# Five matmul rounds instead of six for a channel polynomial, and GpSimd products over two images at once, in a convolution and attention kernel

## The chip, the cores and the metric

The kernel runs on one core of a Trainium2 chip. The metric is the device time of one execution in microseconds. TensorE multiplies matrices into PSUM, VectorE and ScalarE read and write PSUM and SBUF, GpSimd works on SBUF alone, and SyncE (SP) issues DMAs. All data is float32.

## The reference

Two layers over 32 images of 64 channels and 56 x 56 pixels (3136 pixels, called N).

Layer 0 works in 8 groups of 8 channels. In each group, at each pixel, it forms all products of two channels (36) and of three (120), and mixes each set with a learned matrix:

```python
p2 = x[:, :, _I2] * x[:, :, _J2]
y2 = jnp.einsum('bgihw,goi->bgohw', p2, W2).reshape(B, Ch, H, Wd) + b2[None, :, None, None]
p3 = x[:, :, _I3] * x[:, :, _J3] * x[:, :, _K3]
y3 = jnp.einsum('bgihw,goi->bgohw', p3, W3).reshape(B, Ch, H, Wd) + b3[None, :, None, None]
return inp + y2 * beta2 + y3 * beta3 * CONV3_SCALE
```

Layer 1 is an attention over pixels, with a small convolution behind it:

```python
g = jnp.clip(_bn(conv1x1(l, w_inside), ...), 0.0, 6.0)
theta = l[:, :c_red]                            # 32 of the 64 channels
f = jnp.einsum('niab,nicd->nabcd', theta, theta)
f = softmax(f, over the first pixel index); f = softmax(f, over the second)
out = jnp.einsum('nabcd,nicd->niab', f, g) / h * w
out = _bn(depthwise_conv3x3(out, w_dw), ...)
return out + l
```

## The kernel before

**Pairs and tiles.** The images go two at a time, in 16 pairs (`NP`). The 64 channels of image 0 and of image 1 of a pair lie on the two halves of the 128 partitions of `y`, three of which are kept in turn (`ys`). The 3136 x 3136 attention matrix of an image is made in tiles of 128 rows (`QT`), 24 for each image and one for the two remainders: 49 tiles a pair (`IT`), 784 in all. The loop at the end of the kernel body runs over tiles `t`. A tile has two halves. `scores(t, half)` multiplies `theta` with itself into four PSUM banks (tile `ps`, a single buffer), and VectorE copies the half to `e` in SBUF, with a running minimum in `nm`. ScalarE then takes the exponential of the whole tile (`first_softmax`), and of that once more (`second_softmax`, one tile later). Three tiles later (`LAG`), `attend` multiplies the rows of `e` with `g` (tiles `gq`, `gx`) into the accumulators `av` and `ax`: 25 blocks of two matmuls, `split(t)` of them in the first half of a tile, the others in the second.

**The polynomial as matmuls.** The host stores each group's channels in rotated order and extends them (`EXT` rows), so that "channel i + d" of all channels is one load that starts d rows further on. A product of two channels, one d apart, needs two such loads and an elementwise multiply; all pairs with the same d (an orbit) are then a product of 32 partitions (8 channels of 4 groups, half an image). Four orbits stand above one another on 128 partitions (`NSLOT`), and one matmul contracts them all. `STEPS` lists, for each slot, the quadratic orbit a and the cubic ones that go with it. For a piece of half an image (index `k`, 0 to 3 for the four halves of a pair) round 0 contracts `q = x0 * xa` (the four quadratics), rounds 1 to 4 contract `q` times the loads "0", "2", "4" and "b" (the cubics). The last quadratic orbit, channels 4 apart, has no slot left: it is a sixth round of its own (`NRND` is 5, so `r == NRND`), from the loads `c`, multiplied by GpSimd over both images, 128 partitions, with the weights `w4`.

**Chunks.** The pixels of a pair go in 13 chunks of 242 (`PCS`, the last one of 232). In `products`, GpSimd multiplies, for each chunk and `k`, one product of 128 x 242 a round (20 in all), and one for `c`. The products land in rings (`ring_q`, `ring_pr`; `ROOM`), and the loads come from rings `x0`, `xs`, `xc` (`XB`), which SP fills in the order of `plan`, as far as slots are free (`held`) and as `PACE` allows. The first image (two halves) is made before the loop by VectorE, in seven chunks of 448 columns (`first_loads`, `first_products`, `first_poly`), and the second image of the first pair (`TWO`) in the loop, in chunks of 484 columns (`DCS`), one half image at a time.

**Units beside the attention.** While pair n is attended to, the polynomial of pair n + 1 is computed. `rounds` cuts the rounds of a chunk into units: two rounds a unit (`per`), three in the stretch of `TWO`. `poly` issues a unit's matmuls into a free part of the bank `ax`; behind the last unit `poly_out` adds bias and input on VectorE, to `y`. `g_unit` makes a part of `g` in the same place. Each unit has a half tile (`hs`), and a weight of 1 + 3.6 for each round; `split` gives the half with less of such work more attention blocks. The 3 x 3 convolution of pair n - 1 is done by VectorE at the same time: 45 steps (`conv_step`, `scalar_tensor_tensor` over `tt` and `y`) in half tiles in which no unit ends (`leaves`). GpSimd adds a bias ahead of each block of it (`conv_begin`).

**Order.** Each engine runs its instructions in the order of the program (`Pinned`). Waits between engines are put in from the tiles that are read and written. All matmuls, products and loads stand on one line of the profile, L110 (L111 in the kernel after).

Of the kernel before, what the change touches and what calls it, by code (L numbers as in the profile page):

```python
# [19 lines left out]
N = H * W  # L20
# [31 lines left out]
    (0, [0, 2, 4, 5]),  # L52
    (1, [0, 2, 4, 1]),
    (2, [0, 2, 4, 5]),
    (3, [0, 2, 4, 1]),
# [3 lines left out]
NRND = 5  # L59
NPROD = sum(1 + len(bs) for _, bs in STEPS)  # L60
# [11 lines left out]
def tile_poly_conv_attention(  # L72
# [60 lines left out]
    w4 = const.tile([128, 128], FP, name="w4")  # L133
    at = 0
    for s, (_, bs) in enumerate(STEPS):
        for h in range(2) if s < NSLOT else ():
            act.dma_start(
                out=wq[s::NSLOT, :, h, :],
                in_=wpoly[h * 32 : h * 32 + 32, at : at + NRND, h * 32 : h * 32 + 32],
            )  # L140
        if s == NSLOT:
            act.dma_start(out=w4, in_=wpoly[:, at, :])
        at += 1 + len(bs)
# [14 lines left out]
    for k in range(2):  # L158
        pe.matmul(
            out=ax[:, k * 256 : k * 256 + 256],  # L160
            lhsT=w4,
            rhs=wq.rearrange("p k h o -> p (k h o)")[:, :256],
            start=(k == 0),
            stop=True,
            skip_group_check=True,
        )
# [39 lines left out]
    def parts(tiles):  # L206
# [10 lines left out]
        "0": [(0, 1, 0, 0)],  # L217
        "a": [(0, 1, 0, 1)],
        "2": [(0, 1, 2, 0)],
        "4": [(0, 1, 4, 0)],  # L220
        "b": [(0, 2, 5, 0), (1, 2, 1, 0)],
    }

    def first_loads(c):
        p0, w = FCS[c]

        def load(dst, k, d, grow, steps):
            src = bass.AP(x.tensor, (k * EXT + d) * 4 * N + p0, [[N, 32], [grow * 4 * N, steps], [1, w]])
            if steps == 1:
                src = bass.AP(x.tensor, (k * EXT + d) * 4 * N + p0, [[N, 32], [1, w]])  # L230
            (act if fat["q"] % 2 else sync).dma_start(out=dst, in_=src)
            fat["q"] += 1

        fxs[c] = {}
        for name, k in [(a, k) for k in (0, 1) for a in "0a"] + [(a, k) for a in "24b" for k in (0, 1)]:
            t = fx[fat["x"] % len(fx)]
            fat["x"] += 1
            fxs[c][name, k] = t
            for s0, every, d, grow in LOADS[name]:
                load(t[s0::every, :] if every > 1 else t, k, d, grow, NSLOT // every)  # L240
        for d in (0, 1):
            t = fx[fat["x"] % len(fx)]
            fat["x"] += 1
            fxs[c]["c", d] = t[:C, :]
            for k in (0, 1):
                load(t[k * 32 : k * 32 + 32, :], k, 4 * d, 0, 1)

    def first_products(c):
        xs = fxs[c]

        def product(a, b):
            p = fp[fat["p"] % len(fp)]
            fat["p"] += 1
            dve.tensor_tensor(p, a, b, ALU.mult)
            return p

        q = {k: product(xs["0", k], xs["a", k]) for k in (0, 1)}
        frs[c] = [q] + [{k: product(q[k], xs[a, k]) for k in (0, 1)} for a in "024b"]
        dve.tensor_tensor(xs["c", 1], xs["c", 0], xs["c", 1], ALU.mult)
        frs[c].append(dict.fromkeys((0, 1), xs["c", 1]))  # L260
# [8 lines left out]
    for k in range(NRND):  # L269
        by = row("beta2_0") if k == 0 else b3row  # L270
        w = wq[:, k, :, :].rearrange("p h o -> p (h o)")
        dve.tensor_tensor(w, w, by, ALU.mult)
    for half in (0, C):
        w = w4[:, half : half + C]
        dve.tensor_tensor(w, w, row("beta2_0"), ALU.mult)
# [25 lines left out]
    XB = {"x0": 6, "xs": 14, "xc": 3}  # L301
# [12 lines left out]
    ringc = xp.tile([128, 2 * XB["xc"] * PCH], FP, name="ring_xc", tag="xc", bufs=1)  # L314
# [7 lines left out]
    def take_ring(tag, w):  # L322
        t, at = ring[tag]
        m, size = many(w), t.shape[1]
        if at % m or at + m > size:
            at = 0
        ring[tag][1] = (at + m) % size
        return t[:, at : at + m, :].rearrange("p m w -> p (m w)")[:, :w]

    def load_next():  # L330
        tag, key = plan.pop(0)
        n, c, ks, name, k = key
        p0, w = chunks(ks)[c]
        if name[0] == "c":
            held[tag] += 1
            sub = int(name[1:])
            p0, w = p0 + sub * PCH, min(PCH, w - sub * PCH)
            o = fat["c"] % XB["xc"] * 2 * PCH
            fat["c"] += 1
            t = ringc[:, o : o + 2 * PCH].rearrange("p (d w) -> p d w", d=2)  # L340
            at = slice(ks[0] * 32, ks[-1] * 32 + 32)
            for d in range(2):
                src = bass.AP(
                    x.tensor,
                    ((4 * n + ks[0]) * EXT + 4 * d) * 4 * N + p0,
                    [[EXT * 4 * N, len(ks)], [N, 32], [1, w]],
                )
                start(t[at, d, :w], src)
            loaded[key] = [t[at, d, :w] for d in range(2)]
            return  # L350
        held[tag] += many(w)
        t = take_ring(tag, w)
        for s0, every, d, grow in LOADS[name]:
            src = bass.AP(
                x.tensor,
                ((4 * n + k) * EXT + d) * 4 * N + p0,
                [[N, 32], [grow * 4 * N, NSLOT // every], [1, w]],
            )
            start(t[s0::every, :] if every > 1 else t, src)
        loaded[key] = t  # L360

    def prefetch():
        while plan and credit[0] >= 1:
            tag, (_, c, ks, _, _) = plan[0]
            m = 1 if tag == "xc" else many(chunks(ks)[c][1])
            if held[tag] + m > XB[tag]:
                return
            load_next()
# [6 lines left out]
    def products(n, c, ks):  # L375
# [5 lines left out]
        m = many(w)  # L381

        def use(name, k=None):
            key = n, c, ks, name, k
            return loaded.pop(key)

        x0 = {}
        rounds = [{}]
        both = []
        prods[n, c, ks] = rounds, both  # L390
        yield "q", m * len(ks)
        for k in ks:
            yield "load", (n, c, ks, "a", k)
            x0[k] = use("0", k)
            xa = use("a", k)
            q = take_ring("q", w)
            pool.tensor_tensor(q, x0[k], xa, ALU.mult)
            rounds[0][k] = q
            held["xs"] -= m
            prefetch()  # L400
        for r, of in enumerate(("0", "2", "4", "b")):
            rounds.append({})
            yield "pr", m * len(ks)
            for k in ks:
                if of != "0":
                    yield "load", (n, c, ks, of, k)
                xr = x0[k] if of == "0" else use(of, k)
                p = take_ring("pr", w)
                pool.tensor_tensor(p, rounds[0][k], xr, ALU.mult)
                rounds[-1][k] = p  # L410
                held["x0" if of == "0" else "xs"] -= m
                prefetch()
        at = slice(ks[0] * 32, ks[-1] * 32 + 32)
        yield "pr", m
        p4 = take_ring("pr", w)[at, :]
        for sub in range(m):
            yield "load", (n, c, ks, f"c{sub}", None)
            both.append(use(f"c{sub}"))
            pool.tensor_tensor(p4[:, sub * PCH : min((sub + 1) * PCH, w)], *both[sub], ALU.mult)
        rounds.append({k: p4 for k in ks})  # L420
# [26 lines left out]
    def feed(n, c, ks):  # L447
        todo = [("x0" if name == "0" else "xs", name, k) for k in ks for name in "0a"]
        for name in "24bc":
            if name == "c":  # L450
                todo += [("xc", f"c{sub}", None) for sub in range(many(chunks(ks)[c][1]))]
            else:
                todo += [("xs", name, k) for k in ks]
        for tag, name, k in todo:
            plan.append((tag, (n, c, ks, name, k)))
# [18 lines left out]
    def poly(n, c, ks, rs, sub):  # L474
# [4 lines left out]
        at = slice(ks[0] * 32, ks[-1] * 32 + 32)  # L479
        for r in rs:  # L480
            for k in ks:
                pe.matmul(
                    out=ax[k * 32 : k * 32 + 32, AUX : AUX + w],
                    lhsT=wq[:, r, k % 2, :] if r < NRND else w4[at, k * 32 : k * 32 + 32],
                    rhs=rounds[r][k][:, px],
                    start=False,
                    stop=(r == NRND),
                    skip_group_check=True,
                )
            if ends:  # L490
                taken["pr" if r else "q"] -= (sub + 1) * (1 if r == NRND else len(ks))

    def poly_out(n, c, ks, sub):
# [4 lines left out]
        xc = prods[n, c, ks][1][sub][0]  # L498
# [210 lines left out]
    def make_diags():  # L709

        eye = take_ring("xs", 128)
# [5 lines left out]
        for k in range(9):  # L717
            t = take_ring("xs", 128)
# [82 lines left out]
    def poly_unit(n, c, ks, rs, sub, hs):  # L801
        ends = rs[-1] == NRND
# [29 lines left out]
    def first_poly(c):  # L832
        p0, w = FCS[c]
        for r in range(NRND + 1):
            for k in (0, 1):
                pe.matmul(
                    out=banks[c][k * 32 : k * 32 + 32, :w],
                    lhsT=wq[:, r, k, :] if r < NRND else w4[:C, k * 32 : k * 32 + 32],
                    rhs=frs[c][r][k],
                    start=(r == 0),  # L840
                    stop=(r == NRND),
# [3 lines left out]
    def first_out(c):  # L845
        p0, w = FCS[c]
        dve.scalar_tensor_tensor(
            ys[0][:C, p0 : p0 + w], banks[c][:C, :w], bias0[:C], fxs[c]["c", 0], ALU.add, ALU.add
        )
# [68 lines left out]
    for n in range(NP):  # L918
# [4 lines left out]
        def rounds(m, c, ks, per):  # L923
            return [
                ("p", m, c, ks, list(range(r, r + per)), sub)
                for sub in range(many(chunks(ks)[c][1]))
                for r in range(0, NRND + 1, per)
# [202 lines left out]
```

## Time and profile before

| | us |
|---|---|
| device time, median of 3 runs | 4951.68 (4951.55 to 4952.49) |
| profiled execution, span | 4946.9 |
| TensorE busy | 4722.0 (95%) |
| ScalarE busy | 4553.9 (92%) |
| VectorE busy | 4120.5 (83%) |
| GpSimd busy | 3208.4 (65%) |
| loop, first pair (start of ScalarE's first tile to the second pair's) | 381.5 |
| loop, pairs 1 to 14, each | 293.3 to 294.0 |
| loop, last pair | 282.0 |

The profiled execution's own time is its span with what lies around it; the span is 4.8 us shorter than the median. A row of the profile names engine, operation, the tiles written and read (out<-in, without buffer numbers), partitions x elements, the number of instructions, their busy time (overlaps counted once) and the mean duration of one. A float32 matmul leaves two records. Matmuls on different columns of the array overlap, so the busy time of a group divided by its count is less than the duration of one.

### The profile page before, as it was taken

The page shows a single profiled execution, that of the slowest core. Times are in us where ns is not written, and L with a number is a line of the kernel's source. Part 1 is how long each engine was busy: PE and PEld are TensorE (multiplying, and loading weights), DVE is VectorE, ACT ScalarE, POOL GpSimd, SP SyncE. Part 2 cuts the span into 40 slices and gives each one's busy share as a digit, 9 for nine tenths or more (in the row PEclk, how much of TensorE's full clock was granted, in tenths as well). Part 3 has the DMA queues.
Part 4 walks back from the last instruction along what each step waited for, and adds up shares of the span by engine and source line. Part 5 has one row for each costly group of instructions (what it writes and reads, how often), then busy time and mean ns, then how long its engine had stood idle before and what let it go on. Part 6 is the DMA issues. An engine that isn't in the chain of part 4 may idle for free.

```text
span 4946.9 us, 263995 instructions
## 1 busy us (share of the span) xinstructions
PE 4722.0 (95%) x118122; PEld 3215.6 (65%) x118122; DVE 4120.5 (83%) x6100; ACT 4553.9 (92%) x2356; POOL 3208.4 (65%) x4275
## 2 busy tenths in 40 slices
PE   4998999999999999999999999999999999999887
PEld 1555666666666666666666666666666666666665
DVE  4655898888988898888889889888888889888887
ACT  0777899999999999999999999999999999999996
POOL 1777685858758586785858768585875858678000
PEclk8999999999999999999999999999999999999999
DMA  6555656565565655556565555656555565554201
GB/s 203 152 148 153 146 144 155 145 151 141 138 145 145 152 147 143 147 145 144 149 145 147 147 146 142 150 145 152 146 140 141 150 147 146 145 147 125 45 11 34
DMA packets 875486, 685.65 MB, mean 139 GB/s; under 512 B 289772, under 2 KB 860524, under 8 KB 870252
## 3 DMA queue, kind: packets, MB, share of 16 engines
q1 hardware_dynamic: 865964, 657.85, 52.0%
q8 instruction: 924, 15.14, 1.3%
q10 hardware_dynamic: 8384, 10.91, 0.7%
q14 instruction: 214, 1.75, 0.1%
HBM read 565.65 MB, written 25.69 MB: 120 GB/s over the span
## 4 chain that ended last, share of the span: by engine, by line
PE 78%; DVE 11%; issue 3%; DMA 3%; ACT 3%; POOL 1%; SPq 1%; ACTq 0%; DVEq 0%; POOLq 0%
PE av L110 33%; PE ps L110 26%; PE ax L110 19%; DVE e L110 9%; ACT e L110 3%; DMA ring_xs<-in_x_dram 2%; POOL ring_pr L110 1%; DVE y L110 1%; DVE num L110 1%; SPq L110 1%; DMA ring_xc<-in_x_dram 1%; DMA first<-in_x_dram 1%; PE first_s L110 0%; DMA th<-y 0%; POOL ring_q L110 0%
## 5 line engine op out<-in xcount | busy, mean ns | idle before, releaser
L110 PEld LDWEIGHTS av<-gq,e 128*64 128x64 f32 x64512 | 2011.4, 138 | 943.1 <-issue 936.1
L110 ACT ACTIVATE e<-e,nm 128x3136 f32<-128x3136 f32 x784 | 2282.9, 2912 | 235.2 <-DVE e L110 219.6
L110 ACT ACTIVATE e<-e,rz 128x3136 f32<-128x3136 f32 x784 | 2270.3, 2896 | 0.0
L110 PE MATMUL av<-gq,e 128*64 128x65 f32 x64512 | 2224.2, 225 | 3.1 <-ACT e L110 3.0
L110 POOL TENSOR_TENSOR ring_pr<-ring_q,ring_xs 128x242 f32<-128x242 f32 (+2 forms) x2382 | 1784.5, 783 | 533.7 <-PE ax L110 522.8
L110 DVE TENSOR_SCALAR_CACHE_REDUCE e<-ps 128x1568 f32<-128x1568 f32 x784 | 1403.8, 1791 | 321.1 <-PE ps L110 301.7
L110 DVE TENSOR_SCALAR_CACHE_REDUCE e<-ps,nm 128x1568 f32<-128x1568 f32 x784 | 1448.3, 1847 | 254.1 <-PE ps L110 249.1
L110 PE MATMUL ps<-th 32*64 32x392 f32 x25088 | 1453.5, 515 | 131.6 <-DVE e L110 112.3
L110 POOL TENSOR_TENSOR ring_pr<-ring_q,ring_x 128x242 f32<-128x242 f32 (+2 forms) x794 | 606.2, 789 | 607.4 <-PE ax L110 574.8
L110 DVE SCALAR_TENSOR_TENSOR y<-tt,wdt,y 128x605 f32<-128x605 f32 (+6 forms) x711 | 708.2, 996 | 6.4 <-DMA tt<-tr 5.2
L110 PEld LDWEIGHTS ps<-th 32*64 32x64 f32 x25088 | 370.4, 130 | 476.8 <-DVE e L110 382.4
L110 POOL TENSOR_TENSOR ring_q<-ring_x,ring_xs 128x242 f32<-128x242 f32 (+2 forms) x794 | 570.3, 745 | 169.3 <-DMA ring_xs<-in_x_dram 166.4
L110 PE MATMUL ax<-gq,e 128*64 128x65 f32 x12288 | 490.3, 222 | 0.0
L110 PE MATMUL ax<-ring_pr,wq 128*32 128x242 f32 (+1 forms) x6448 | 474.5, 373 | 2.2 <-POOL ring_pr L110 1.1
L110 PEld LDWEIGHTS ax<-gq,e 128*64 128x64 f32 x12288 | 425.5, 138 | 0.3
L110 PEld LDWEIGHTS ax<-ring_pr,wq 128*32 128x32 f32 x6448 | 177.0, 109 | 106.9 <-POOL ring_pr L110 13.3
L110 POOL TENSOR_SCALAR y<-y,bias 128x616 f32<-128x616 f32 (+2 forms) x79 | 145.4, 1842 | 98.9 <-PE ax L110 98.9
L110 DVE SCALAR_TENSOR_TENSOR y<-ax,bias,ring_xc 128x242 f32<-128x242 f32 (+3 forms) x208 | 97.0, 467 | 102.6 <-PE ax L110 102.6
L110 PE MATMUL ax<-wit,y 128*64 128x64 f32 x3136 | 143.3, 223 | 31.1 <-issue 17.9
L110 POOL TENSOR_TENSOR ring_pr<-ring_xc 128x242 f32<-128x242 f32 (+3 forms) x208 | 127.7, 615 | 67.8 <-DMA ring_xc<-in_x_dram 59.2
L110 ACT ACTIVATION_READ_ACCUMULATOR e<-e,nm 128x1 f32 x784 | 145.4, 185 | 0.0
L110 PEld LDWEIGHTS ax<-wit,y 128*64 128x64 f32 x3136 | 118.9, 139 | 37.0 <-issue 18.7
(86 smaller groups left out, 1388.4 us busy)
## 6 DMA issues: line engine op xcount, KB each, us to landing
ring_xs<-in_x_dram SPq DMA_DIRECT2D x2184, 121.0 KB
ring_x<-in_x_dram SPq DMA_DIRECT2D x720, 121.0 KB
ring_xs<-in_x_dram SPq DMA_DIRECT2D x1440, 60.5 KB
th<-y SPq DMA_DIRECT2D x124, 392.0 KB
ring_xc<-in_x_dram SPq DMA_DIRECT2D x360, 121.0 KB
ring_xs<-in_x_dram SPq DMA_DIRECT2D x186, 116.0 KB
out_dram<-y SPq DMA_DIRECT2D x60, 308.0 KB
tt<-tr SPq DMA_DIRECT2D x128, 100.0 KB
```

The costliest lines, as they stand in the source:

```text
L110: i = f(*args, **kw)
```

## The change

The orbits are dealt out anew over the slots, so that slot 2 has only three cubic rounds. Its place in round 2 (`SR`, `SS`) takes the last quadratic: GpSimd writes `x0` times the load "2" (in slot 2 that is the channel 4 further on) over the 32 partitions of that slot in the round's product. The sixth round, its loads, its product and `w4` go; `c` loads now only the input that `poly_out` adds. Slots lie in blocks of 32 partitions instead of every fourth one. The load "a" is used in round 1 too and is held that long; `x0` is held to round 2, and its ring has 8 slots instead of 6, while `xc` has half the size. In chunks of all four halves, GpSimd multiplies two halves in one instruction (`pieces`): 128 x 2 x 242. Units are of rounds 0 and 1, 2 and 3, and 4 (0 to 2, and 3 and 4, in the stretch of `TWO`). VectorE makes the partial product in the first image.

```diff
 STEPS = [
-    (0, [0, 2, 4, 5]),
-    (1, [0, 2, 4, 1]),
-    (2, [0, 2, 4, 5]),
-    (3, [0, 2, 4, 1]),
+    (0, [0, 2, 4, 1]),
+    (1, [1, 3, 4, 2]),
+    (2, [2, 4, 3]),
+    (3, [3, 5, 4, 0]),
     (4, []),
 ]
+SR, SS = 2, 2
...
     LOADS = {
-        "0": [(0, 1, 0, 0)],
-        "a": [(0, 1, 0, 1)],
-        "2": [(0, 1, 2, 0)],
-        "4": [(0, 1, 4, 0)],
-        "b": [(0, 2, 5, 0), (1, 2, 1, 0)],
+        "0": [(0, 4, 0, 0)],
+        "a": [(0, 4, 0, 1)],
+        "2": [(0, 4, 2, 1)],
+        "4": [(0, 4, 4, 0)],
+        "b": [(0, 3, 1, 1), (3, 1, 0, 0)],
     }
+    SPARE = slice(SS * 32, SS * 32 + 32)
...
-    XB = {"x0": 6, "xs": 14, "xc": 3}
+    XB = {"x0": 8, "xs": 14, "xc": 3}
...
+    def pieces(ks):
+        return [(0, 1), (2, 3)] if len(ks) == len(ALL) else [(k,) for k in ks]
...
         yield "q", m * len(ks)
-        for k in ks:
-            yield "load", (n, c, ks, "a", k)
-            x0[k] = use("0", k)
-            xa = use("a", k)
-            q = take_ring("q", w)
-            pool.tensor_tensor(q, x0[k], xa, ALU.mult)
-            rounds[0][k] = q
-            held["xs"] -= m
+        for pc in pieces(ks):
+            yield "load", (n, c, ks, "a", pc)
+            x0[pc] = use("0", pc)
+            xa[pc] = use("a", pc)
+            q[pc] = take_ring("q", w, pc)
+            pool.tensor_tensor(q[pc], x0[pc], xa[pc], ALU.mult)
             prefetch()
-        for r, of in enumerate(("0", "2", "4", "b")):
-            rounds.append({})
+        done(q)
+        for r, of in enumerate("a24b", 1):
+            p = {}
             yield "pr", m * len(ks)
-            for k in ks:
...
+            for pc in pieces(ks):
+                if of != "a":
+                    yield "load", (n, c, ks, of, pc)
+                xr = xa[pc] if of == "a" else use(of, pc)
+                p[pc] = take_ring("pr", w, pc)
+                pool.tensor_tensor(p[pc], q[pc], xr, ALU.mult)
+                if r == SR:
+                    pool.tensor_tensor(p[pc][SPARE], x0[pc][SPARE], xr[SPARE], ALU.mult)
+                    held["x0"] -= m * len(pc)
+                held["xs"] -= m * len(pc)
                 prefetch()
-        at = slice(ks[0] * 32, ks[-1] * 32 + 32)
-        yield "pr", m
-        p4 = take_ring("pr", w)[at, :]
         for sub in range(m):
             yield "load", (n, c, ks, f"c{sub}", None)
             both.append(use(f"c{sub}"))
-            pool.tensor_tensor(p4[:, sub * PCH : min((sub + 1) * PCH, w)], *both[sub], ALU.mult)
-        rounds.append({k: p4 for k in ks})
...
-                    lhsT=wq[:, r, k % 2, :] if r < NRND else w4[at, k * 32 : k * 32 + 32],
+                    lhsT=wq[:, r, k % 2, :],
                     rhs=rounds[r][k][:, px],
...
-                ("p", m, c, ks, list(range(r, r + per)), sub)
+                ("p", m, c, ks, list(range(r, min(r + per, NRND))), sub)
                 for sub in range(many(chunks(ks)[c][1]))
-                for r in range(0, NRND + 1, per)
+                for r in range(0, NRND, per)
```

## The prediction

> **What bounds the kernel now.** I read the page first (busy shares), then the waits of the regular stretch, then TensorE's timeline of single tiles, then the rows of GpSimd's products. The page:
>
> ```profile
> PE 4722.0 (95%) x118122; PEld 3215.6 (65%) x118122; DVE 4120.5 (83%) x6100; ACT 4553.9 (92%) x2356; POOL 3208.4 (65%) x4275
> ```
>
> TensorE is busy for 95% and ScalarE for 92%: a saving on the first soon meets the second. Who waits for whom from 810 to 4600 us:
>
> ```profile
> POOL ring_pr L110 <- PE ax L110: 979.2, 328, 29.0
> ...
> DVE e L110 <- PE ps L110: 335.8, 691, 1.1
> PEld ps L110 <- DVE e L110: 294.1, 709, 1.0
> ```
>
> GpSimd waits for TensorE to free its rings, 979 us in all, and no row has TensorE waiting for GpSimd. TensorE and VectorE wait for each other: the score banks are single, so scores, their copy by VectorE, and the next scores are one chain. Two half tiles without side work show its floor (TensorE's timeline; start, duration, what):
>
> ```profile
> 1950.37 0.92 PE L110 MATMUL ps<-th 32*64 32x392 f32 x16
> ...
> 1953.25 0.92 PE L110 MATMUL ps<-th 32*64 32x392 f32 x16 [0.41 <-DVE e L110]
> ...
> 1956.18 0.92 PE L110 MATMUL ps<-th 32*64 32x392 f32 x16 [0.35 <-DVE e L110]
> ```
>
> 2.88 and 2.93 us, 5.81 together. ScalarE needs as much: 2.91 + 2.90 us for its two exponentials. No tile goes below this. Now the tile with the last two rounds of a chunk, and a g unit in its second half:
>
> ```profile
> 1758.37 0.91 PE L110 MATMUL ps<-th 32*64 32x392 f32 x16
> 1759.22 1.39 PE L110 MATMUL av<-gq,e 128*64 128x65 f32 x40
> 1760.53 0.62 PE L110 MATMUL ax<-ring_pr,wq 128*32 128x242 f32 x8
> 1760.96 0.59 PE L110 MATMUL ax<-ring_pr,w 128*32 128x242 f32 x8
> 1761.49 0.91 PE L110 MATMUL ps<-th 32*64 32x392 f32 x16
> ...
> 1764.58 0.90 PE L110 MATMUL ps<-th 32*64 32x392 f32 x14
> ```
>
> 3.12 + 3.09 = 6.21 us, without a wait: here TensorE's own work is the limit, 0.4 us above the floor. From the first poly matmul to the next scores is 0.96 us for two rounds, 0.48 each.
>
> **The sixth round, regular stretch.** A pair of images has 49 tiles and 13 chunks, each chunk three poly units: rounds 0-1, 2-3, and 4-5, which becomes 4 alone. Only the third changes; the scheduler places it in the same half tile, and `split` gives that half more attention blocks (12 instead of 10; the built order shows 24 of the matmul pairs ahead of it, 48 records). First half: 48 attention records take 1.62 us, plus 0.48 is 2.10, the sum that the half of two rounds beside 32 records has now (1.15 + 0.95), and that lasts 2.88 us (1752.51 to 1755.39). Second half: the halves with 36 + 16 attention records and a g unit last 2.94 us now. So 5.82 instead of 6.21, minus 0.39. Through the 13 third tiles of the pair at 1680 us: six save 0.38; the two whose VectorE copy starts late save 0.28 and 0.22; two that last 6.17 and 6.05 now save 0.34 and 0.22; two without a g unit (5.86, 5.88) save 0.03 each; one, where two transposes hold VectorE, saves nothing. Together 3.4 us a pair, in 14 pairs: minus 48 us. The other 36 tiles keep their work. The removed round's busy time is more (107.7 + 9.0 + 7.2 + 0.6 = 124.5 us by its rows), but what lies above the floor is all that can go.
>
> **Pair 0.** From 125 to 225 us the second image pair's half is computed (images 2, 3), and tiles last 3.74 + 3.98 = 7.72 us, TensorE without a wait. One round of two matmuls, about 0.5 us, leaves each of 14 pieces: minus 6 us, if GpSimd keeps up; per chunk of 484 columns it needs 12 products of 1.18 = 14.2 us (now 13.1) against two tiles of 7.2, so it barely does (bounds 0 and minus 7). From 293 to 470 us TensorE waits for products, and the issue of loads on SP sets the pace:
>
> ```profile
> 335.44 11.30 SPq L110 DMA_DIRECT2D ring_xs<-in_x_dram  x17
> ```
>
> 0.665 us an issue, 26 a chunk, 17.3 us, close to the 17.9 that a chunk takes there. The change loads one `c` piece instead of two and forms no `c` product, for which GpSimd waited some 3 us a chunk: 25 issues, minus 0.67 us by 12 chunks, minus 8 us (bounds minus 2 and minus 18, the latter if the missing wait shortens the loop as well).
>
> **The head.** VectorE forms the first image's products; in five of seven chunks it paces (7.1 us a chunk). Two partial products for one `c` product add 0.55 us (eight of them took 4.37), 2.7 in all; three more weight DMAs sit ahead of the loads on ScalarE's queue, 2 us; two loads of 16 less per chunk give back about 4. Plus 1 (minus 3 to plus 5).
>
> **GpSimd's products.** The rows by form:
>
> ```profile
> L110 POOL TENSOR_TENSOR ring_pr<-ring_q,ring_xs 128x242 f32<-128x242 f32 x2160 | 1604.0, 776 | 498.3 <-PE ax L110 488.5 <-DMA ring_xs<-in_x_dram 6.7 <-DMA ring_xc<-in_x_dram 2.7
> ...
> L110 POOL TENSOR_TENSOR ring_pr<-ring_q,ring_xs 128x484 f32<-128x484 f32 x36 | 42.6, 1227 | 0.0
> ```
>
> Back to back they start 0.66 and 1.18 us apart. A chunk: 20 x 0.66 + 0.6 = 13.9 us now, 10 x 1.18 + 2 partial ones after. A product of 64 partitions took 616 ns, of 128 partitions 617, so I take 1.18 for the 32 partitions too: 14.2 us. GpSimd gains no time. It has it: a chunk's last product now ends 13 to 22 us before TensorE reads it, and a chunk has 17.5 us at the fastest. `a` is held for one round more and loads go in pairs; with the same 14 slots this costs lead, not time. No queue behind SP's waits changes order: `th`, `tt` and stores stand between the same tiles.
>
> **What it adds to VectorE.** Each conv step (two SBUF inputs, 45 a pair) stands ahead of a score copy, that is, on the chain:
>
> ```profile
> 1749.39 0.84 DVE L110 SCALAR_TENSOR_TENSOR y<-tt,wdt,y 128x605 f32<-128x605 f32 x1
> ```
> ```profile
> 1755.12 4.55 POOL L110 TENSOR_TENSOR ring_pr<-ring_q,ring_xs 128x242 f32<-128x242 f32 x5 [2.31 <-PE ax L110]
> ...
> 1755.25 1.22 DVE L110 SCALAR_TENSOR_TENSOR y<-tt,wdt,y 128x605 f32<-128x605 f32 x1
> ```
>
> The first ran with GpSimd idle, the second began 0.13 us into a product: 0.58 us of the product was left, and 1.22 is 0.64 more than that. Over the 360 steps of this form the duration is, but for a few, 0.64 us plus what is left of the running product, and not below 0.82. So today a step loses at most 0.5 us, and the copy behind it, which waits for scores until 1.03 us into the next half, leaves 0.35: overshoots are 0.1 to 0.2, and rare. With products of 1.22 us a step can lose 1.0 and overshoot by 0.67. No row shows a wide product beside a conv step (pair 0 has none), so bounds: nothing, if the phases fall well; 0.19 us mean at a random phase (0.67 squared over 2 x 1.18) by 0.6 busy by 45 steps = 5.1 us a pair. Laid out by hand over the commonest chunk (steps in four halves running, GpSimd released by the end of a poly unit) what is left at each step is 0.2 to 0.4: no loss. Chunks with a gap in their steps meet a fresh product, 0.2 to 0.5 each, some four a pair. I take 1.8 us a pair, 25 in 14 pairs.
>
> The Trainium skill, "SBUF — State Buffer", section "SBUF: two separate sides", says that VectorE with two SBUF inputs and GpSimd share a port pair as an exclusive lock, held for the whole instruction. It speaks against the change: longer products are longer locks. By the lock the sum is the one below; if the two only shared bandwidth, the 25 would be near 0 and the time 4891.
>
> **The sum.** Profiled span 4946.9; the median of the runs is 4.8 above it, which stays. 4951.7 - 48 - 6 - 8 + 1 + 25 = 4916.
>
> **The rivals.** *The port decides* (slower): the gain of 61 us is spread over 630 conv steps, so 0.097 us of mean overshoot eats it. At random phase it is 0.11: 72 - 61 = plus 11, 4963; with half the steps meeting a fresh product (0.5 late), 158 - 61, near 5050. For it: there is no slack on the chain beyond 0.35. Against it: GpSimd's bursts begin at fixed points of the tile. *The port costs nothing*: 4891. *All removed TensorE time comes back*: 4951.7 - 124.5 = 4827; against it stand the 5.82 floor and ScalarE's 5.81. That the round is not removed is excluded by the built order.
>
> **Chances.** Forecast, 4896 to 4941: 0.48. Port free, 4875 to 4896: 0.20. Full time back: 0.02. The port takes nearly all of the gain, 4942 to 4961: 0.07. It decides, above 4961: 0.23. The range 4882 to 4980 leaves out some 0.1 at each end. A difference under 0.2%, 10 us, can't be told from none: faster 0.48 + 0.20 + 0.02 = 0.7, same 0.07, slower 0.23.
>
> **What would show it.** Third tiles at 5.82 instead of 6.21; the other tiles at 5.86; pair 0 near 368 instead of 381 us; partial products near 1.2 us; 605-column steps beside products up to 1.9 us, with score copies late after them. I am wrong if tiles without a third unit grow beyond 6 us, if TensorE waits for `ring_pr` after 510 us, or if the 484-column product in the regular stretch is far from 1.18.

## The result and the profile after

The kernel after takes 6925.17 us (median of 4 runs, 6924.05 to 6929.57), the kernel before 4951.61 us beside it: a ratio of 1.3989, 95% interval 1.3969 to 1.4009. Forecast were 4916 us. The polynomial lost a round, and the kernel takes two fifths more time.

The span grew by 1980.9 us (6927.8 against 4946.9). Starts of ScalarE's first tile in each pair say where: the head grew from 124.4 to 245.7 us, pair 0 from 381.5 to 592.1, each of the pairs 1 to 14 from 293.5 to 411.1. The last pair, in which nothing is loaded for a next one, takes 282.0 us in both. So the time stands where loads run. The page after, with its busy times, the slices and the load queue:

```profile
PE 5095.9 (74%) x116482; PEld 3346.2 (48%) x116482; DVE 4227.6 (61%) x6107; ACT 4552.9 (66%) x2356; POOL 3196.2 (46%) x2521
...
DMA  2232332434233232332434233242333324233211
...
DMA packets 798798, 659.18 MB, mean 95 GB/s; under 512 B 239502, under 2 KB 783886, under 8 KB 793614
...
q1 hardware_dynamic: 790526, 633.17, 31.1%
```

No engine is near its span any more, and the DMA engines are busy for a third. The same queue before, with 4% more bytes:

```profile
q1 hardware_dynamic: 865964, 657.85, 52.0%
```

A low share of all 16 engines looks like a queue with time to spare; it is not, as the experiments show. Who waits for whom from 1400 to 6500 us of the kernel after:

```profile
ACT e L111 <- DVE e L111: 1569.7, 301, 24.4
POOL ring_q L111 <- DMA ring_xs<-in_x_dram: 1527.4, 304, 8.4
PEld ps L111 <- DVE e L111: 1109.0, 649, 19.8
...
DVE y L111 <- POOL y L111: 837.8, 62, 18.8
```

The second line is the head of the chain. GpSimd, which waited 979 us for TensorE before (in 3790 us), now waits 1527 us for loads (in 5100 us). Because it is late, the bias that it adds ahead of a convolution block is late (fourth line); VectorE stands behind that bias, and the score copies behind VectorE. The other lines are read as echoes of it; experiment 1, where they go with it, bears that out. SP's timeline of the loads, start, duration and count:

```profile
3018.09 2.66 SPq L111 DMA_DIRECT2D ring_x<-in_x_dram  x2
3020.85 20.57 SPq L111 DMA_DIRECT2D ring_xs<-in_x_dram  x18
3042.35 0.60 SPq L111 DMA_DIRECT2D ring_xc<-in_x_dram  x1
```

18 issues in 20.57 us are 1.14 us each, where the prediction reckoned with 0.665. GpSimd's products themselves cost nearly what was forecast: wide ones that follow each other start 1.18 us apart (median), and 1.30 us into and out of one of 32 partitions, which lasts as long as a wide one (mean of one in ns behind the bar). A wide product covers two half images, the two halves of one image, and not two images as the title has it.

```profile
L111 POOL TENSOR_TENSOR ring_pr<-ring_q,ring_xs 128x484 f32<-128x484 f32 x1488 | 1886.7, 1281 | 1168.3 <-DMA ring_xs<-in_x_dram 534.3 <-PE ax L111 451.6 <-DMA ring_x<-in_x_dram 87.7
L111 POOL TENSOR_TENSOR ring_pr<-ring_x,ring_xs 32x484 f32<-32x484 f32 x372 | 476.0, 1280 | 29.2
```

### The profile page after: what moved, and what is told of

Same layout as the page of the kernel before. It is cut to its first block, busy times and chain, and to the rows that moved or that the text cites. A ratio compares the mean times of both kernels' runs of the same rounds, so it can differ in the third digit from the quotient of the medians.

```text
span 6927.8 us, 255939 instructions
## 1 busy us (share of the span) xinstructions
PE 5095.9 (74%) x116482; PEld 3346.2 (48%) x116482; DVE 4227.6 (61%) x6107; ACT 4552.9 (66%) x2356; POOL 3196.2 (46%) x2521
## 2 busy tenths in 40 slices
DMA packets 798798, 659.18 MB, mean 95 GB/s; under 512 B 239502, under 2 KB 783886, under 8 KB 793614
## 5 line engine op out<-in xcount | busy, mean ns | idle before, releaser
L111 PEld LDWEIGHTS av<-gq,e 128*64 128x64 f32 x64512 | 2133.7, 145 | 1032.6 <-issue 1024.4
L111 PE MATMUL ps<-th 32*64 32x392 f32 x25088 | 1606.8, 550 | 1368.7 <-DVE e L111 1067.4
L111 POOL TENSOR_TENSOR ring_pr<-ring_q,ring_xs 128x484 f32<-128x484 f32 (+2 forms) x1616 | 2031.5, 1270 | 1201.3 <-DMA ring_xs<-in_x_dram 562.7
L111 PE MATMUL av<-gq,e 128*64 128x65 f32 x64512 | 2350.3, 232 | 4.8 <-ACT e L111 3.0
L111 POOL TENSOR_TENSOR ring_q<-ring_x,ring_xs 128x484 f32<-128x484 f32 (+1 forms) x404 | 501.4, 1241 | 2141.0 <-DMA ring_xs<-in_x_dram 2092.2
L111 DVE SCALAR_TENSOR_TENSOR y<-tt,wdt,y 128x605 f32<-128x605 f32 (+6 forms) x711 | 809.6, 1139 | 956.7 <-POOL y L111 950.0
L111 PEld LDWEIGHTS ps<-th 32*64 32x64 f32 x25088 | 397.1, 137 | 1793.3 <-DVE e L111 1324.0
L111 PE MATMUL ax<-ring_pr,wq 128*32 128x242 f32 (+1 forms) x6448 | 588.8, 391 | 192.3 <-POOL ring_pr L111 189.1
L111 POOL TENSOR_TENSOR ring_pr<-ring_x,ring_xs 32x484 f32<-32x484 f32 (+1 forms) x404 | 519.2, 1285 | 31.7
L111 PE MATMUL ax<-ring_q,wq 128*32 128x242 f32 x1612 | 159.8, 387 | 92.5 <-POOL ring_q L111 91.7
```

Of the source, the lines that this page charges most:

```text
L111: i = f(*args, **kw)
```

## Theories

**Narrow loads.** With slots in blocks of 32 partitions, the source pattern of a load begins with the 4 slots and has the 32 rows inside; before, it began with the 32 rows and had the 4 slots inside. The destination is 128 partitions in both. If a load is spread over as many DMA engines as its first dimension allows, it went over 16 and now goes over 4 (3 for the 96-row part of `b`). **Rivals.** The wide products hold the port and make VectorE and GpSimd late; or the lead is lost (`a` is held longer, loads go in pairs on the same 14 slots).

The trace supports the first by a count of its own. The 16-engine form of experiment 1 has the same DMAs and loads the same bytes as the kernel after, but 288790 packets under 512 B instead of 239502, 49288 more:

```profile
DMA packets 848086, 659.38 MB, mean 135 GB/s; under 512 B 288790, under 2 KB 833174, under 8 KB 842902
```

Say that each share of a load leaves one such packet. The kernel after has 3176 loads of 128 rows in the loop and 56 in the head, at 16 - 4 = 12 shares fewer, and 794 + 14 loads of 96 rows at 16 - 3 = 13 fewer: 3232 x 12 + 808 x 13 = 49288, to the packet. Between the kernel before (289772) and experiment 4, which gives it narrow loads (240484), the difference is 49288 again.

The pace follows. Per chunk the narrow loads put 16 x 32 + 4 x 32 (`b`) + 32 (`c`) = 672 packets of 968 bytes behind each other on the engines they use, the 32-row loads 8 more. At the 45 ns that such a packet takes (the median in both traces; mean 49 after) that is 30.6 to 33.3 us a chunk; measured are 411.1 / 13 = 31.6. Before, 16 x 8 + 8 x 4 + 2 x 32 = 224 packets, 10 to 13 us, fitted into a chunk's 22.6. Counted over the middle fifth of its packets, the load queue of the kernel after is never without a packet in flight, and most often has exactly four (53% of the time); before, anything from none to 19 was in flight, 16 most often (8%).

## Experiments

| | us (median) | ratio to before, 95% | head | pair 0 | pairs 1 to 14, mean |
|---|---|---|---|---|---|
| before | 4951.61 | | 124.4 | 381.5 | 293.5 |
| after | 6925.17 | 1.3969 to 1.4009 | 245.7 | 592.1 | 411.1 |
| 1: after, 16 engines | 4898.44 | 0.9876 to 0.9903 | 120.0 | 334.6 | 293.2 |
| 2: after, 8 engines | 4970.80 | 1.0023 to 1.0053 | 154.2 | 361.8 | 294.3 |
| 3: as 1, narrow products | 4934.62 | 0.9947 to 0.9974 | 123.4 | 360.2 | 293.2 |
| 4: before, 4 engines | 7191.71 | 1.4492 to 1.4545 | 254.9 | 620.5 | 427.1 |
| 5: before, rows stacked | 4928.28 | 0.9932 to 0.9961 | 122.2 | 361.5 | 293.6 |
| 6: as 1, three chunks narrow | 4890.09 | 0.9855 to 0.9887 | 122.8 | 343.6 | 292.0 |
| 7: as 1, merged loads | 4895.03 | 0.9868 to 0.9897 | 117.7 | 329.8 | 293.9 |
| 8: 6 and 7 together | 4892.21 | 0.9860 to 0.9889 | 117.9 | 342.6 | 292.9 |
| 9: as 1, chunks 7 to 9 narrow | 4874.75 | 0.9831 to 0.9861 | 123.5 | 336.7 | 291.3 |
| 10: as 1, no partial product | 4927.42 | 0.9936 to 0.9966 | 120.0 | 331.3 | 295.7 |
| 11: 1 again | 4901.12 | 0.9882 to 0.9915 | 122.6 | 338.8 | 293.2 |

Ratios are to the kernel before as it was run beside each; head and pairs are those of the profiled execution.

**1, 2, 4: the width of the loads alone.** In 1 the host stores, for each load, its rows one behind the other, and the source becomes one run; 2 puts a pad row behind every 16 rows; 4 gives the kernel before the block layout of the kernel after (slots, weights, source patterns, and the further rotated rows that its load "b" then needs) and nothing else. In 1, 2 and 3 load "a" reads channels 1 to 4 in place of 0 to 3, as many rows and bytes, so that their output is that of another polynomial; 6 to 11 read the right ones. The edits shown are shortened, with constants put in.

```diff
 (1)
-src = bass.AP(x.tensor, ..., [[grow * 4 * N, steps], [N, 32], [1, w]])
+src = bass.AP(x.tensor, at, [[N, 32 * steps], [1, w]])
 (2)
+src = bass.AP(x.tensor, at, [[17 * N, 2 * steps], [N, 16], [1, w]])
 (4, in the kernel before)
-src = bass.AP(x.tensor, ..., [[N, 32], [grow * 4 * N, steps], [1, w]])
+src = bass.AP(x.tensor, ..., [[grow * 4 * N, steps], [N, 32], [1, w]])
-        "0": [(0, 1, 0, 0)],
+        "0": [(0, 4, 0, 0)],
...
```

Expected of 1:

> The kernel after, with the same instructions, the same 25 loads a chunk and the same bytes; only the rows of x lie otherwise in DRAM: the rows of one load stand one behind the other, so that its source is one run of 128 (or 96) rows instead of 4 (or 3) groups of 32. Theory (narrow loads): a load whose source pattern begins with 4 is served by 4 DMA engines; with 128 ahead it is served by 16. Then SP issues one in 0.55 to 0.6 us as before instead of 1.15 to 1.6, TensorE stops waiting for ring_pr, and the time is what the prediction's sum without the loads says: 4880 to 4930 us, a pair near 290 instead of 413 us, pair 0 near 370 instead of 592. Rival 1 (the wide products and the port): 484-column products hold VectorE's steps and GpSimd is late: nothing changes, 6900 to 6950. Rival 2 (lost lead: a held longer, loads in pairs on 14 slots): nothing changes either, above 6800.

Expected of 2:

> As the run before, but with a pad row behind every 16 rows in DRAM, so that the source pattern of a 128-row load begins with 8 (that of a 96-row load with 6). Narrow loads: twice as many engines as in the kernel after, half as many as in the other run: 16 packets an engine at the 45 ns median of the packets' rows, 0.72 us a load, so SP's back-to-back issues stand 0.7 to 0.8 us apart. 25 of them are 17.5 to 20 us, under the 22.5 us that a chunk has in the regular stretch, above what pair 0 allows: a pair near 290 us, pair 0 20 to 50 us longer than with 16 engines, 4900 to 4990 us. If the order of the rows in DRAM or the length of the run were what counts, the pace of issue would be as in the kernel after or as in the 16-engine one, not between. Rivals of products or lead: above 6800.

Expected of 4:

> The kernel before, with its six rounds, its 242-column products and its c product, but with the slots in blocks of 32 partitions and so source patterns that begin with 4 (3 for the larger load of b), as in the kernel after. Narrow loads: SP's issues of 128-row loads back to back 1.15 to 1.6 us, 26 a chunk at the 1.27 us mean of the kernel after (413 us by 13 chunks by 25 issues) is 33 us a chunk: a pair 415 to 440 us, the whole 6900 to 7300. If products, partial products or lead are the cause: 4950, unchanged.

All three fell where the narrow loads put them: 4898 instead of 6925 us by the order of rows in DRAM alone, 4971 at half the width, and 7192 for the old kernel with narrow loads. The rivals, which expected no change in any of them, are out. Nor is it the length of a run of rows in DRAM: 2 has runs of 16 rows, the kernel after runs of 32, and 2 is the faster. Pair 0 of 1 is shorter than expected (334.6 us, not near 370); experiment 5 takes that up. SP's timeline, one line each of 1 (from its second run, 11), 2 and 4, the first two in pair 0:

```profile
331.19 10.21 SPq L117 DMA_DIRECT2D ring_xs<-in_x_dram  x18
```
```profile
335.88 11.83 SPq L117 DMA_DIRECT2D ring_xs<-in_x_dram  x18
```
```profile
3000.86 15.78 SPq L110 DMA_DIRECT2D ring_xs<-in_x_dram  x11
```

0.57, 0.66 and 1.43 us an issue: only the last, by 26 loads, is more than the 22.6 us of a chunk. The small packets agree again:

```profile
DMA packets 814151, 659.24 MB, mean 133 GB/s; under 512 B 254855, under 2 KB 799239, under 8 KB 808967
```

2 has 33935 fewer of them than 1; 8 shares fewer for 3232 loads and 10 fewer for 808 are 33936. In 2 most often eight packets are in flight. How an average hides a full queue shows in one stretch of each trace (last columns: granted clock, DMA share, GB/s), first the kernel after, then the kernel before:

```profile
2000.00:4000.00 2000.00, 1504.91 (x35500) 1003.65 (x35500) 1282.79 (x1828) 1384.62 (x717) 994.73 (x776) 0.87 0.34 100
```
```profile
1300.00:3000.00 1700.00, 1667.19 (x42752) 1150.27 (x42756) 1480.88 (x2165) 1649.68 (x855) 1201.89 (x1604) 1.00 0.57 146
```

A share of 0.34 is 5.4 engines of 16 on average, in a queue that is never empty.

The Trainium skill, "DMA: Bandwidth & Descriptors", section "Why a DMA increments its semaphore by 16 and not by 1", gives the rule: the number of engines is the largest k up to 16 that divides the slowest dimension of both sides; and among that page's rules for kernel authors stands that an outermost dimension under 16 confines a DMA to at most that many engines. Both agree with the packet counts above (4, 3, 8, 6 and 16 shares). It is the rule that spoke against this change.

**5: how much is the layout's?** The kernel before, with its rows stacked in the same way (its loads had 16 engines already).

```diff
-[[N, 32], [grow * 4 * N, NSLOT // every], [1, w]]
+[[N, 32 * (NSLOT // every)], [1, w]]
```

> The kernel before, with nothing changed but the order of x in DRAM: the rows of each load stand one behind the other in the order of its partitions, so that a source is one run of 128 (or 64) rows instead of 32 groups of 4 (or 2). It asks how much of the 54 us by which the 16-engine form of the kernel after beats the kernel before is the layout's and how much is the change's. There pair 0 took 334.6 us (before 381.5) and a pair of the regular stretch 293.1 (before 293.5). If the layout brings it (SP issues in 0.38 to 0.43 us instead of 0.55): pair 0 near 345 us here, the regular pairs unchanged, 4910 to 4925 us. If the five rounds, the wide products and the missing c product bring it: pair 0 stays at 375 to 382 us, 4945 to 4952 us.

4928 us, between the two: 24 us of the gain of experiment 1 are the layout's, nearly all in pair 0, where SP's issue of a 128-row load takes 0.38 us (median) from one run against 0.55 from 32 groups of 4. The rest is the change's: 4928.3 less 4898.4 or 4901.1 is 27 to 30 us (24 to 29 by the ratios).

**3: one half image per product.**

```diff
-return [(0, 1), (2, 3)] if len(ks) == len(ALL) else [(k,) for k in ks]
+return [(k,) for k in ks]
```

> The 128-row source of the first run, and GpSimd multiplies one half image per instruction (242 columns) as in the kernel before; the rest is the kernel after. Narrow loads: within 40 us of the first run. The difference prices the wide products by themselves: if the port is held for a whole product, 242-column products free VectorE's conv steps sooner, and this run is up to 25 us (prediction's term) faster; against it, 24 products of 0.66 us take 15.8 us a chunk instead of 14.2, so pair 0 can lose up to 10 us. If the wide products were the cause of 6925: this run near 4950 while the first one stays near 6900.

36 us slower than 1 by the medians (the profiled execution, at 4922.63 us, is the fastest of its five), against the sign that was expected. Pair 0 took 25.6 us more: GpSimd, with 24 narrow products a chunk, was busy for 200.25 of the 210 us from 250 to 460. In the regular stretch the median pair gained 0.7 us (292.3), but single pairs of up to 298.3 us took it back. In these a conv step is held through a row of products that follow each other without a gap. VectorE and GpSimd in the longest tile of pair 6, 9.38 us:

```profile
2156.91 4.81 DVE L117 SCALAR_TENSOR_TENSOR y<-tt,wdt,y 128x605 f32<-128x605 f32 x1
```
```profile
2155.07 2.71 POOL L117 TENSOR_TENSOR ring_q<-ring_x,ring_xs 128x242 f32<-128x242 f32 x4
2157.72 3.37 POOL L117 TENSOR_TENSOR ring_pr<-ring_q,ring_xs 128x242 f32<-128x242 f32 x5
```

The step ends 0.63 us behind the last of these nine products. 18 steps of this run took over 2 us; in the kernel before and in 1 none did.

**Where the removed round went in the regular stretch.** Tile by tile (from ScalarE's first exponential of a tile to that of the next; medians over pairs 1 to 14), 21 tiles of experiment 1 are shorter than before by 3.1 us together. A third unit shows in two of them in turn, 5.92 and 5.81 instead of 6.09 and 5.97; on TensorE's timeline, by which the prediction counted, its tile falls from 6.21 to 5.88. TensorE's timeline of one in experiment 11, one round beside 48 records in the first half, the g unit in the second:

```profile
1710.28 0.91 PE L117 MATMUL ps<-th 32*64 32x392 f32 x16
1711.13 1.62 PE L117 MATMUL av<-gq,e 128*64 128x65 f32 x48
1712.68 0.61 PE L117 MATMUL ax<-ring_pr,wq 128*32 128x242 f32 x8
1713.22 0.91 PE L117 MATMUL ps<-th 32*64 32x392 f32 x16
...
1716.16 0.92 PE L117 MATMUL ps<-th 32*64 32x392 f32 x16
```

5.88 us here. But six others are longer by 2.6 to 2.8 us together: tiles 21, 22, 24, 25, 29 and 42. VectorE and GpSimd in tile 21 of the same run:

```profile
1759.84 1.76 DVE L117 SCALAR_TENSOR_TENSOR y<-tt,wdt,y 128x616 f32<-128x616 f32 x1
1761.53 1.84 DVE L117 TENSOR_SCALAR_CACHE_REDUCE e<-ps,nm 128x1568 f32<-128x1568 f32 x1
```
```profile
1758.54 4.15 POOL L117 TENSOR_TENSOR ring_pr<-ring_q,ring_xs 128x484 f32<-128x484 f32 x3
```

The step, 0.85 us when GpSimd is idle, meets a product that began 0.11 us earlier and lasts 1.21; it takes 1.76, and the score copy starts the moment it ends, too late. This is the prediction's port term, in few tiles and in whole pieces.

**6, 7, 8: narrow products in three chunks; fewer loads.**

```diff
 (6)
+SINGLE = (5, 6, 7)
-return [(0, 1), (2, 3)] if len(ks) == len(ALL) else [(k,) for k in ks]
+return [(0, 1), (2, 3)] if len(ks) == len(ALL) and c not in SINGLE else [(k,) for k in ks]
 (7)
-        "b": [(0, 3, 1, 1), (3, 1, 0, 0)],
+        "b": [(0, 4, 1, 1)],
-start(t[s0 * 32 : (s0 + ns) * 32, i, :], src)
+start(t, bass.AP(x.tensor, at, [[N, 128], [ROWS_X * N, 2], [1, w]]))
```

Expected of 6:

> The 16-engine form of the kernel after, with 242-column products in chunks 5, 6 and 7 of every pair and 484-column ones in the others. In the 16-engine run the third tiles came down to 5.81 and 5.92 us as predicted, but seven tiles beside the products of chunks 5, 6, 7 and 11 (tiles 21, 22, 24, 25, 29 and 42 of a pair above all) grew to 6.05 to 6.72, where conv steps took 1.40 to 1.80 us beside 484-column products. Theory (port): in chunks 5 to 7 a narrow product lets a step go sooner, these tiles return to 5.85 to 5.95, 2.4 us a pair by 14 pairs is 34 us: 4855 to 4875 us. Rival (the tiles grow by something else, the attention blocks or the order of the units): they stay long, 4890 to 4905. Third: the 24 narrow products of these chunks make GpSimd late, as in the all-narrow run (tiles 18 and 41 at 6.9 to 7.1): 4880 to 4910 with new long tiles.

Expected of 7:

> The 16-engine form of the kernel after, with fewer and larger loads: the two parts of b in one, both halves of a wide product in one DMA of 256 rows (242 KB), c from one run of 128 rows. 11 loads a chunk instead of 25, all on 16 engines. If SP's issues still pace pair 0 (0.5 us each with what lies between them, 12.5 us a chunk against tiles of two per chunk near 12 us): pair 0 falls from 334.6 to 315 to 328 us, the regular pairs stay, 4880 to 4892 us. If they no longer do, no change: 4895 to 4902. If larger loads land too late for the products: GpSimd waits for ring_xs in pair 0, up to 20 us slower.

Expected of 8:

> The two runs before together: narrow products in chunks 5 to 7, and merged loads (one DMA for two halves where the product is wide). If both effects stand by themselves, the sum of the two: 34 plus 6 to 18 us below the 16-engine form, 4840 to 4860 us.

6 gained 8 us instead of 34, because the chunks were counted wrongly: the long tiles 21 to 29 stand beside the products of chunks 7, 8 and 9. Tiles 21 to 24, beside chunk 7, came right; 25 came right beside wide products that begin at another phase; 29 did not (6.38), and a new one came, tile 18 at 6.80 (median): a step of up to 2.52 us, held through several narrow products that follow each other without a gap. Pair 0 lost 9 us to the narrow products, as in 3. Experiment 7 made no difference that can be told from 1: pair 0 is 5 to 9 us shorter than in 1 and 11, the regular pairs 0.8 longer. So with wide loads SP's issues, 11 a chunk instead of 25, set little of the pace. Experiment 8 brings no more than 6, over 30 us above what was expected.

**9: the right chunks, and none in pair 0.**

```diff
+SINGLE = (7, 8, 9)
+... and (n < 2 or c not in SINGLE) else ...
```

> As the run with narrow products in three chunks, with the chunks counted rightly: the products run two chunks ahead of what was counted there, so that the long tiles 21 to 30 of the 16-engine form stand beside chunks 7, 8 and 9 of the next pair. Those have 242-column products here, from the second pair on; in pair 0, where narrow products cost GpSimd time (343.6 us against 334.6), all are wide. Port theory: tiles 21, 22, 24, 25, 29 and 30 at 5.82 to 5.92 us, as in the all-narrow run, tiles 18 and 41 as in the 16-engine run; 2.6 us a pair by 14 pairs is 36 us: 4858 to 4872 us, a pair near 290.5. Rival (the tiles grow whatever the products' width): 4890 to 4900.

4874.75 us, ratio 0.9846 (0.9831 to 0.9861): faster than both kernels and than experiment 1. The median pair is 290.9 us, tiles 22, 24, 25, 29 and 30 are at 5.82 to 5.92 as expected; tile 21 still takes 6.26, tiles 32 and 35 grew by 0.1 and 0.2 in exchange, and one pair of 295 us has a step of 3.67 us, held through three wide products in a row; together that is more than the 3 us that it missed. In tile 24 a step still starts 0.1 us into a product and takes 1.25 us, where one in experiment 11 took 1.78: there the width decides. Tiles 22, 25 and 29 changed width and phase at once, and tile 21 stays long beside narrow products, so width is not all.

**10: without the partial product; 11: experiment 1 with load "a" on its own channels.**

```diff
 (10)
 if r == SR:
-    pool.tensor_tensor(p[pc][SPARE], x0[pc][SPARE], xr[SPARE], ALU.mult)
 (11, against 1)
-BEGIN = {"0": 0, "a": 4, "2": 5, "4": 9, "b": 13}
+BEGIN = {"0": 0, "a": 3, "2": 5, "4": 9, "b": 13}
```

Expected of 10:

> The 16-engine form of the kernel after without the partial product of 32 partitions, which GpSimd forms twice a chunk for the last quadratic orbit (the slot keeps the wide product's values, so the output leaves that orbit out). It prices the partial product: 2 x 1.2 us of GpSimd a chunk. In the regular stretch GpSimd has time to spare; what can change is which product a conv step meets: a pair 291 to 294 us. In pair 0 the products cost time: 24 chunk halves lighter by 1.2 us, at most 334.6 less 29, more likely 320 to 330. Together 4875 to 4895 us. If the partial product costs nothing on the path: 4895 to 4902.

Expected of 11:

> The 16-engine form of the kernel after, all products of full chunks wide, with load a reading its own channels 0 to 3 (in the first three runs it read channels 1 to 4, the same number of rows and bytes). Nothing in the work differs: 4893 to 4902 us, as the first run, and the base for the two runs beside it.

11 came at 4901 us, as expected. 10 is 26 us slower than 11, although GpSimd does less, and against both things expected of it. Pair 0 gained 7.5 us, the regular pairs lost 2.6 each. Eleven tiles of a pair are now longer than before by 0.45 to 0.81 us, nearly all with a step that starts 0.12 us into a product. VectorE and GpSimd in one of them:

```profile
1708.07 1.76 DVE L117 SCALAR_TENSOR_TENSOR y<-tt,wdt,y 128x605 f32<-128x605 f32 x1
1709.75 1.84 DVE L117 TENSOR_SCALAR_CACHE_REDUCE e<-ps,nm 128x1568 f32<-128x1568 f32 x1
```
```profile
1707.95 5.87 POOL L117 TENSOR_TENSOR ring_pr<-ring_q,ring_xs 128x484 f32<-128x484 f32 x4 [2.63 <-PE ax L117]
```

GpSimd runs out of ring space, TensorE releases it at a fixed point of the tile (the 2.63 us of idle time end there), and it starts 0.12 us ahead of the step. With the partial products in between, the phase is another one. So less work on GpSimd cost 26 us: in this run the price is set by where a product begins, not by how much there is to multiply.

## Why the prediction was wrong

**The step that failed** is the cost of the loads. The prediction gave each of them SP's pace of issue, 0.665 us, and counted one issue less a chunk, minus 8 us. The new order of the slots, in blocks of 32 partitions, it put at nothing: no term of the sum and none of the rivals stands for it. With it the source pattern changed, and with the pattern the number of engines; the 25 issues became 31.6 us a chunk, in every pair for which loads run (117.6 us more in each of the pairs 1 to 14). The trace of before had a row that hinted at it: the `c` load has a source that begins with 4 in both kernels, and in the chain of waits it took twice as long as an `xs` load of the same 121 KB (how much of that is the queue ahead of it the row does not say):

```profile
310.51 5.33 DMA ring_xc<-in_x_dram
316.80 2.68 DMA ring_xs<-in_x_dram
```

With 32 packets in a row at 45 ns instead of 8, the 21 narrow loads of a chunk, with 8 packets of the others, make 13 x 30.6 = 398 us a pair: with the rule cited above that sum could have been made beforehand, 13 us from what was measured. "If TensorE waits for `ring_pr` after 510 us" stood among the signs of an error; it came true (243.9 us of waits of its weight loads alone) by a cause that was not among the rivals. That the time fell above 4961 us, where the port had a chance of 0.23, is no success of that rival.

The other terms can be read where the loads are wide (experiments 1 and 11 against 5 and before):

- **Third tiles.** Forecast minus 3.4 us a pair, measured minus 3.1; on TensorE's timeline 5.82 us forecast, 5.88 found. Right.
- **The port.** Forecast plus 1.8 us a pair, measured 2.6 to 2.8: mechanism right, size too small. Together with the term above nearly nothing is left: minus 0.4 us a pair instead of 1.6. The layout by hand, "no loss" at the commonest chunk, was right; the chunks that "meet a fresh product" are six tiles at up to 0.8 each, not four at 0.2 to 0.5. That a step waits for one product at most, on which the term rests, held in 11, but not in 3 and 9. Experiment 10 is what the slower rival described, a step against a fresh product in most chunks: 5.7 us a pair of it, 79 us, inside its 72 to 158.
- **Pair 0.** The part of the second image, 19 tiles, forecast minus 6: tiles of 7.72 became 7.19, 131.9 us became 127.0 to 127.7. Right within its bounds. The issue-bound part, the other 30 tiles, forecast minus 8 (to minus 18): 229.5 us in experiment 5, 207.6 to 211.1 in 1 and 11, minus 18 to 22. Undersized; how it divides between the missing `c` product (GpSimd waited 18.7 us for `c` in experiment 5 and no longer in 11) and the one issue less was not separated.
- **GpSimd.** 1.18 us was right for wide products that follow each other, 1.30 was found beside a partial one: some 14.6 us a chunk by these spacings, not 14.2. "It gains no time" was a comparison with before; against narrow products in the new scheme the wide ones save pair 0 some 25 us (experiment 3).
- **Head.** Forecast plus 1; 120.0 and 122.6 us against 122.2 with the same loads. Within its bounds.

With wide loads for both kernels, the change is worth 27 to 30 us; the prediction's sum was 36. That the two are near is partly luck: the regular stretch brought 4 to 6 us of the 23 that the sum has for it, and pair 0 9 to 13 more than its 14.

## What to carry to other kernels

Write down the source and the destination pattern of every DMA that an edit touches, first dimension first: a new order of partitions is a new pattern in DRAM, and it can cut the number of engines at the same bytes and the same count. Here 128 rows were 8 packets in a row on each of 16 engines, 16 on 8 and 32 on 4. A low DMA share next to engines that wait for loads was a sign of that here, and the count of packets under 512 B told how many shares a load had. Where VectorE and GpSimd meet on a chain, look at what stands at the place of the meeting: a shorter GpSimd instruction there helped (experiment 9), a row of short ones without a gap cost more than a long one (experiment 3), and less work elsewhere moved the phase and made it worse (experiment 10).

## What was not expected of the hardware

- SP's issue of a 128-row load of 121 KB took 0.38 us (median; experiments 3 and 5) to 0.43 (1 and 11) from one run of 128 rows, 0.55 from 32 groups of 4 and 0.60 from 8 groups of 16, though two of these use 16 engines and one 8; from 4 groups of 32 it took 1.22.
- The granted clock of TensorE was lower where it waited for work: 0.87 in the stretch shown of the kernel after, 1.00 before. 67 of the 239 tiles of that stretch still took 5.81 us; what the clock did to the others was not separated.
- A conv step that starts within a product mostly goes ahead of the next one, but at times it is held through a whole row of products without a gap: 4.81 us in experiment 3 and 2.52 in experiment 6 (narrow), 3.67 in experiment 9 (three wide), against 1.80 beside one wide product. What decides between the two is not shown.
